# A four-layer attention network on one Trainium2 core: in layer 0 the product with v and the output projection take turns by steps, and the product for the sums moves one step behind GpSimd's addition

## The chip, the cores and the metric

The kernel runs on one core of a Trainium2 chip. The core has five engines that work side by side: TensorE (PE in the profile, its weight loads PEld), VectorE (DVE), ScalarE (ACT), GpSimd (POOL) and SyncE (SP, which here only issues transfers). Each runs its own instructions in the order of the program and waits where it needs the result of another. The metric is the device time in microseconds of one execution. The kernel before has a median of 2780.14 us in three runs.

## What is computed

A batch of four images with 512 channels and 32 x 32 pixels (1024 tokens) passes through four residual layers. Layers 0 and 2 are attention, layer 1 a gate per channel, layer 3 a lookup of the eight nearest rows of a table. The change is in layer 0, for each image:

```python
q, k, v = w_q @ gn(x), w_k @ gn(x), w_v @ gn(x)          # 8 heads of 64 channels
attn = einsum('bhdq,bhdT->bhqT', q, k) * scale           # scores per head
attn = einsum('gh,bhqT->bgqT', w_head, attn)             # mix the heads
attn = softmax(attn, axis=-1)
attn = (attn - mean) / sqrt(var + EPS) * gamma + beta    # norm of each head's whole map
out = einsum('bhqT,bhdT->bhqd', attn, v)
out = out.reshape(b, t, c) @ w_proj.T + b_proj
x = x + out
```

All data are 32-bit floats.

## The kernel before

**Steps.** Layer 0 walks over the images b = 0 to 3, and each image over steps s (the function `step`). An image has STEPS = 32 blocks of 32 queries. Step s does four things on four different blocks: it multiplies q and k for block s (`scores`, L425, in two halves), mixes the heads of block s - 2 (`mix`, L445), takes the exponent and turns it (`exps` L452, `turn_keys` L458), and multiplies with v a group of four blocks that lies LAG = 6 steps back (`apply`, L485). An image runs 38 steps: 32, and six in which only the later stages go on while the next image's q is projected. With `j, part = divmod(s - 6, 4)` a group j of four blocks (128 queries) is multiplied with v in the four steps part = 0 to 3: a quarter of the keys in each, all into the PSUM bank `pv`. After part 3 `take_out` (L548, ACT) copies the bank out.

**The relay.** Between scores and mix the rows must change partitions. After the second half of the scores ACT has copied them to `ss` (L431), and eight transfers, four issued by SP and four by GpSimd (L438), carry them to `s2`, which the mix two steps later reads. The page calls this transfer s<-ss.

**The sums.** The softmax denominators come from statistics that DVE takes of every exponent tile (`reduce`, bn_stats at L474). For a group j the generator `sums` does, in this order, one stretch per call of `next`: GpSimd adds up the statistics (L506); TensorE multiplies by the constant matrix `same`, which sums over partitions (L509), and DVE takes the reciprocal `ri` (L512); GpSimd stores `ri` to DRAM (L517) and checks its range; GpSimd loads it back spread over the partitions as `rb` (L525) and squares the statistics; GpSimd finishes the sum of squares `ssq`. The generator is held in `I["tail"]`. Before, the calls fall in part 0 at the head of the step, part 0 after the scores, and the ends of parts 0, 1 and 2. At the end of part 3 the generator `scale` starts: GpSimd multiplies the copied bank by `rb` (L561, half at the end of part 3, half at the end of the next part 0), and SP stores the result at the end of the next part 1.

**The projection of the image before.** While image b > 0 is in steps OUT = 12 to 27, `piece` projects the output of image b - 1: `put_quarter` makes in each step 256 columns of one of four row blocks (four matmuls at L658), DVE adds bias and residual (`add_to`, L624), and every second quarter closes a piece of 512 columns (`piece_done`, L640). 16 quarters make an image. The image's rows come by `image_piece` in odd steps and leave by `piece_out` in even steps.

**One shared bank.** `small_ps` always returns the same PSUM bank, pt. The projection of v (`take_v`, steps 0 to 6), the row sum of v (`sum_v`, L395 in step 7 and L405 in step 8), the product for the sums, the output projection, the statistics of the next image (`prepare` through `group_coeffs_parts`, L140 and L150) and the gate of layer 1 (`gating`, L815 and others, from step 28) all use it in turn; each waits until the one before has been read out.

**Order.** Nearly every instruction goes through `pin`, which keeps the order of the program on its engine. So the order of TensorE in a step is the order of the calls in `step`: scores, mix, scores, then (part 0) the product for the sums, `mid` (which calls sum_v, prepare or gating), `apply`, `piece`.

Of the kernel before, what the change touches and what calls it, by code (L numbers as in the profile page):

```python
# [16 lines left out]
P = 128  # L17
# [5 lines left out]
NB = 512  # L23
# [18 lines left out]
def fast_net(ctx: ExitStack, tc: tile.TileContext, a: dict, out: bass.AP, flag: bass.AP):  # L42
# [13 lines left out]
    def pin(ins):  # L56

        return tc.keep_in_program_order(ins)

    def small_ps(name):  # L60
        return pt_bank
# [154 lines left out]
    LAG = 6  # L216
# [151 lines left out]
    def take_k(b, m, at):  # L368
        I = img[b]
        if m == 0:  # L370
            I["k"] = big("k", f"k0_{b}")
        project(I["w_k"], tokens(I["xn"]), m, at,
                lambda ps: pin(nc.vector.tensor_copy(
                    I["k"][:, m, :].rearrange("p (t b j) -> p t j b", t=4, j=NS),
                    ps.rearrange("p (t j b) -> p t j b", t=4, j=NS))))

    def take_v(b, t):

        I = img[b]
        if t == 0:  # L380
            I["v"] = big("v", f"v0_{b}").rearrange("p k (i c) -> p (k i) c", c=C)
        ps = small_ps(f"v_{b}_{t}")
        for k in range(KC):
            pin(nc.tensor.matmul(  # L384
                ps, I["xn"][:, k, t::TC], I["w_v"][:, k, :],
                start=(k == 0), stop=(k == KC - 1),
            ))
        pin(nc.scalar.copy(I["v"][:, t, :], ps))
# [25 lines left out]
    def scores(b, s, n):  # L414


        I = img[b]
        q, k_ = I["q"], I["k"]
        if n == 0:
            I["ss", s] = eight_k([P, 2, T], f"ss_{b}_{s}", s % 2)  # L420
        ss = I["ss", s]
        sc = pairs["sc"]
        for m in range(KC):
            for r in range(2):
                pin(nc.tensor.matmul(  # L425
                    sc[m * NS:(m + 1) * NS, r, :],
                    q[r * HD:(r + 1) * HD, m, s * NS:(s + 1) * NS],
                    k_[r * HD:(r + 1) * HD, m, n * NB:(n + 1) * NB],
                    start=True, stop=True,
                ))  # L430
        pin(nc.scalar.copy(ss[:, :, n * NB:(n + 1) * NB], sc))  # L431
        if n == 0:
            return
        s2 = I["s2", s] = apool.tile([P, 2, T], F32, tag="s2", bufs=2, name=f"s2_{b}_{s}")
        del I["ss", s]
        for m in range(KC):
            for r in range(2):
                pin(relays[r].dma_start(  # L438
                    out=s2[r * KC + m::NH], in_=ss[m * NS:(m + 1) * NS, r, :]))

    def mix(b, s):
        s2 = img[b].pop(("s2", s))
        for t in range(4):
            for r in range(4):
                pin(nc.tensor.matmul(  # L445
                    pairs[f"mx{r // 2}"][t * NS:(t + 1) * NS, r % 2, :].rearrange("p (qq k) -> p qq k", qq=2),
                    wmix[r * NS:(r + 1) * NS], s2[r * NS:(r + 1) * NS, :, t * NK:(t + 1) * NK],
                    start=True, stop=True,
                ))

    def exps(s, half):
        pin(nc.scalar.activation(  # L452
            e[:, half].rearrange("p r qq k -> p (r qq k)"), flat2(pairs[f"mx{half}"]), AF.Exp))

    def turn_keys(s, half):

        j, i = divmod(s, 4)
        pin(nc.vector.transpose(  # L458
            eT[:, j % 2].rearrange("p b (qq i r) x -> p i r qq b x", qq=2, i=4)[
                :, i, 2 * half:2 * half + 2],  # L460
            e[:, half].rearrange("p r qq (b x) -> p r qq b x", x=NS),
        ))
# [10 lines left out]
                for qq in range(2):  # L473
                    pin(nc.vector.bn_stats(st[:, i, 2 * half + r, qq, :], e[:, half, r, qq, :]))  # L474

    def apply(b, s):

        I = img[b]
        j, part = divmod(s, 4)
        pv = pv_bank.rearrange("p (gp q) -> p gp q", q=P)  # L480
        for t in (2 * part, 2 * part + 1):
            for gp in range(KC):
                for r in range(2):
                    g = 2 * gp + r
                    pin(nc.tensor.matmul(  # L485
                        pv[r * HD:(r + 1) * HD, gp, :],
                        I["v"][:, t, g * HD:(g + 1) * HD],
                        eT[:, j % 2, t, :, 4 * g:4 * g + 4],
                        start=(t == 0 and gp == 0), stop=(t == TC - 1),
                        skip_group_check=True,  # L490
                    ))
# [54 lines left out]
    def take_out(b, j):  # L546
        pv = img[b]["pv"] = apool.tile([P, KC, P], F32, tag="o1", name=f"pv_{b}_{j}")
        pin(nc.scalar.copy(pv.rearrange("p gp q -> p (gp q)"), pv_bank))  # L548
# [66 lines left out]
    def out_view(b):  # L615
        return img[b]["of"].rearrange("p (j k g x) -> p k g j x", j=TC, g=NH, x=NS // 2)
# [6 lines left out]
    def add_to(b, m, xr, ps):  # L623
        pin(nc.vector.scalar_tensor_tensor(  # L624
            xr, ps, bproj[:, m:m + 1], xr, ALU.add, ALU.add))
# [5 lines left out]
    def piece_done(b, m, n):  # L631

        I = img[b]
        xr = I["xr", m, n]
        if n == 0:
            I["stb"] = small.tile([P, 2, 6], F32, tag="bnst", name=f"st_b{b}_{m}")
        if n == 0 and m == 0:
            I["mv"] = small.tile([P, KC, 2], F32, tag="mv", name=f"mv_b{b}")
        st, mv = I["stb"], I["mv"]
        pin(nc.vector.bn_stats(st[:, n, :], xr))  # L640
        if n == 0:
            return
        pin(nc.vector.bn_aggr(mv[:, m, :], st.rearrange("p i s -> p (i s)")))
        if m == KC - 1:
            mv1 = I["mv1"] = const.tile([P, 2, KC], F32, tag=f"mv1_{b}", name=f"mv1_{b}")
            pin(nc.vector.tensor_copy(mv1[:, 0, :], mv[:, :, 0]))
            pin(nc.vector.tensor_copy(mv1[:, 1, :], mv[:, :, 1]))

    def put_quarter(b, i):


        I = img[b]
        m, n4 = divmod(i, 4)
        Q = NB // 2
        ps = small_ps(f"p_{b}_{i}")[:, 0:Q]
        o = out_view(b)
        for k in range(KC):
            pin(nc.tensor.matmul(  # L658
                ps, I["w_p"][:, k, m * P:(m + 1) * P], o[:, k, 2 * n4:2 * n4 + 2],
                start=(k == 0), stop=(k == KC - 1),  # L660
            ))
        add_to(b, m, I["xr", m, n4 // 2][:, n4 % 2 * Q:(n4 % 2 + 1) * Q], ps)
        if n4 % 2:
            piece_done(b, m, n4 // 2)

    def put_out(b, m, at):

# [454 lines left out]
    for m, at in enumerate(("mx1", "sc", "mx0", "mx1")):  # L1122
        take_k(0, m, at)

    def step(b, s, mid, piece):


        I = img[b]
        old = s - 2
        j, part = divmod(s - LAG, 4)  # L1130
        tiled = 0 <= j < TC
        if tiled and part == 0:
            I["tail"] = sums(b, j)
            next(I["tail"])
        if s == 0:
            take_v(b, 0)
        if s < STEPS:
            scores(b, s, 0)
            early(b, s)
        if 0 <= old < STEPS:  # L1140
            mix(b, old)
            exps(old, 0)
            turn_keys(old, 0)
        elif s < STEPS:
            piece(b, s)
        if s < STEPS:
            scores(b, s, 1)
        if 0 <= old < STEPS:
            exps(old, 1)
        if tiled and part == 0:  # L1150
            next(I["tail"])
        mid(b, s)
        if tiled:
            apply(b, s - LAG)
            if part == 3:
                take_out(b, j)
        if 0 <= old < STEPS:
            turn_keys(old, 1)
            reduce(b, old)
        if old >= 0:  # L1160
            piece(b, s)
        if tiled and part < 3:
            next(I["tail"], None)
        if tiled and part < 2 and j > 0:
            next(I["scale"])
        if tiled and part == 3:
            I["scale"] = scale(b, j)
            next(I["scale"])

    OUT, NEXT = 12, 28
    state = {"behind": iter(()), "load": iter(())}

    def early(b, s):

        if b > 0 and s == TC - 1:
            state["load"] = collect(b - 1, False)
        if s == NEXT:
            state["load"] = (  # L1180
                next_image(0, "Wq", x1[0]) if b + 1 == B else next_image(b + 1, "w_q", x_v[b + 1]))
        next(state["load"], None)
# [22 lines left out]
    def piece(b, s):  # L1205
        if s < TC - 1:
            take_v(b, s + 1)
        elif b > 0 and OUT <= s < OUT + 16:
            put_quarter(b - 1, s - OUT)
        if TC < s < NEXT - 3 and not state["held"]:  # L1210
            state["held"] = next(state["ahead"]) is True

    for b in range(B):
# [4 lines left out]
        for s in range(STEPS):  # L1218
            step(b, s, mid, piece)
# [85 lines left out]
    for s in range(len(tiles) + 3):  # L1305
        if s < len(tiles):
            b, tt = tiles[s]
# [735 lines left out]
```

## Time and profile before

| what | value |
|---|---|
| median of three runs | 2780.14 us (2775.45 to 2785.22) |
| span of the profiled execution | 2784.4 us |
| TensorE busy over the span | 2614.6 us, 94% |
| stretch 465 to 580 us (image 1, steps with the projection): PE, DVE, ACT, POOL busy of 115 us | 111.68, 96.73, 66.80, 67.07 |
| the same stretch: share of the DMA engines, rate | 0.81, 211 GB/s |
| stretch 130 to 330 us (image 0, steps 6 and on, no projection): PE, DVE, ACT, POOL busy of 200 us | 178.19, 149.16, 115.81, 122.87 |
| the same stretch: share of the DMA engines, rate | 0.73, 190 GB/s |

The page's shares over the whole span mix four layers. For a change in layer 0 one reads the stretches of layer 0 (roughly 76 to 1310 us) and asks in each what the next matmul waited for. An fp32 matmul shows as two records, so "x8" in a line of L658 is four matmuls. A transfer's row shows its issue; when it landed is seen only in the chain of waits, from the instruction that it released.

### The profile page before, as it was taken

The numbers are of one execution on the slowest core, as the hardware profiler recorded it, in microseconds if no ns is written. First come the engines' busy times: TensorE is split into PE (matmuls) and PEld (weight loads), VectorE is DVE, ScalarE is ACT, GpSimd is POOL, SyncE is SP. The second block draws the span as 40 slices with busy tenths as digits, with TensorE's granted clock in tenths as the row PEclk, the third lists the DMA queues.
The fourth block names the chain that finished last, engine by engine and source line by source line (L and its number), as shares of the span: only waits on it lengthen the run. The fifth ranks groups of instructions, "written<-read, shape, count | busy, mean of one in ns | idle before, by whom it ended". The sixth has DMA issues, their size and how long they took to land.

```text
span 2784.4 us, 46982 instructions
## 1 busy us (share of the span) xinstructions
PE 2614.6 (94%) x18286; PEld 1170.4 (42%) x18286; DVE 1530.0 (55%) x2407; ACT 1003.6 (36%) x1128; POOL 1253.2 (45%) x1947
## 2 busy tenths in 40 slices
PE   7998998989989898989999999999999999999995
PEld 3443444545445443545433433343343334444442
DVE  4488347871578426872245234514623446888876
ACT  0465336551565325551154024214502532121210
POOL 2266415552456415562066026305601635666664
PEclk9999999999999999999999999999999999999997
DMA  2477438880687537784300030021002006766665
GB/s 77 107 205 205 140 90 213 218 214 27 161 222 209 151 82 196 194 216 173 127 18 1 31 121 1 16 76 60 1 30 91 1 28 192 217 185 213 186 185 149
DMA packets 159321, 349.82 MB, mean 126 GB/s; under 512 B 32361, under 2 KB 65129, under 8 KB 155378
## 3 DMA queue, kind: packets, MB, share of 16 engines
q1 hardware_dynamic: 86304, 167.04, 20.8%
q0 software_dynamic: 51200, 142.93, 19.0%
q10 hardware_dynamic: 21586, 36.76, 4.6%
q8 instruction: 147, 2.41, 0.4%
q14 instruction: 84, 0.69, 0.1%
HBM read 178.57 MB, written 33.69 MB: 76 GB/s over the span
## 4 chain that ended last, share of the span: by engine, by line
PE 74%; DMA 9%; ACT 6%; DVE 4%; POOL 4%; issue 3%; SPq 1%; ACTq 0%; POOLq 0%; DVEq 0%
PE at L1057 16%; PE mx L183 7%; PE sc L425 7%; PE pv_c L971 6%; PE pv L485 6%; PE sc_c L939 5%; DMA s<-ss 5%; PE pt L384 4%; PE sc L183 4%; ACT ss L431 3%; PE k L183 3%; PE v L195 3%; PE q L183 3%; PE p L183 3%; PE pt L658 3%
## 5 line engine op out<-in xcount | busy, mean ns | idle before, releaser
L458 DVE STREAM_TRANSPOSE eT<-e 128x1024 f32<-128x1024 f32 x256 | 317.4, 1242 | 278.5 <-ACT e L452 276.6
L438 POOL DMA_DIRECT2D s<-ss x512 | 260.4, 516 | 391.0 <-ACT ss L431 316.0
L947 ACT ACTIVATE eT<-sc_c 128x1024 f32<-128x1024 f32 x256 | 248.1, 1021 | 359.2 <-PE sc_c L939 357.2
L1074 POOL DMA_INDIRECT got<-in_mem,ix x256 | 278.9, 1089 | 209.9 <-issue 113.0
L431 ACT COPY ss<-sc 128x1024 f32<-128x1024 f32 x256 | 258.9, 1011 | 262.0 <-PE sc L425 203.0
L474 DVE BATCH_NORM_STATS2 st<-e 128x6 f32<-128x256 f32 x1024 | 341.6, 406 | 0.0
L425 PE MATMUL sc<-k,q 64*32 64x512 f32 x4096 | 286.3, 614 | 21.5 <-ACT ss L431 16.3
L955 POOL TENSOR_TENSOR e<-eT 128x1024 f32<-128x1024 f32 x96 | 232.4, 2423 | 149.3 <-ACT eT L947 139.0
L452 ACT ACTIVATE e<-mx 128x1024 f32<-128x1024 f32 x256 | 262.5, 1028 | 69.6 <-PE mx L445 35.8
L956 DVE TENSOR_TENSOR eT<-eT,e 128x1024 f32<-128x1024 f32 x96 | 143.5, 1494 | 236.3 <-POOL e L955 236.1
L485 PE MATMUL pv<-eT,v 128*64 128x128 f32 x4096 | 258.9, 281 | 0.0
L939 PE MATMUL sc_c<-q,k 64*128 64x512 f32 x1024 | 254.4, 615 | 3.7 <-DVE xr L624 2.3
L485 PEld LDWEIGHTS pv<-eT,v 128*64 128x64 f32 x4096 | 228.5, 140 | 62.1 <-issue 60.5
L971 PE MATMUL pv_c<-eT,v 128*64 128x512 f32 x1024 | 248.1, 605 | 2.8 <-ACT eT L947 2.8
L445 PE MATMUL mx<-s,wmix 32*32 32x512 f32 x4096 | 160.5, 630 | 51.1 <-DMA s<-ss 50.0
L1098 DVE SCALAR_TENSOR_TENSOR acc<-got,et,acc 128x512 f32<-128x512 f32 x224 | 168.5, 752 | 8.0
L996 DVE RECIPROCAL ri_c<-ri_c 128x512 f32<-128x512 f32 x32 | 107.2, 3351 | 112.5 <-ACT ri_c L995 112.5
L939 PEld LDWEIGHTS sc_c<-q,k 64*128 64x128 f32 x1024 | 88.3, 186 | 152.4 <-issue 127.6
L952 POOL TENSOR_TENSOR eT<-eT 128x1024 f32<-128x1024 f32 x32 | 78.9, 2466 | 146.2 <-ACT eT L947 146.2
L1000 POOL DMA_DIRECT2D fcw<-ri_c x64 | 33.3, 522 | 247.3 <-DVE ri_c L996 243.0
L561 POOL TENSOR_TENSOR o<-pv,rb 64x256 f32<-64x256 f32 x128 | 111.4, 870 | 73.3 <-ACT pv L548 66.4
L1062 ACT COPY att<-at 128x1024 f32<-128x1024 f32 x64 | 64.8, 1012 | 217.7 <-PE at L1057 194.4
(314 smaller groups left out, 3336.2 us busy)
## 6 DMA issues: line engine op xcount, KB each, us to landing
s<-ss SPq DMA_DIRECT2D x512, 128.0 KB
s<-ss POOLq DMA_DIRECT2D x512, 128.0 KB
rb<-r POOLq DMA_DIRECT2D x64, 128.0 KB
o<-o SPq DMA_DIRECT2D x32, 256.0 KB
xr<-in_x ACTq DMA_DIRECT2D x32, 256.0 KB
x<-xr SPq DMA_DIRECT2D x32, 256.0 KB
xr_c<-x SPq DMA_DIRECT2D x32, 256.0 KB
x<-xr_c SPq DMA_DIRECT2D x32, 256.0 KB
```

The costliest lines, as they stand in the source:

```text
L183: pin(nc.tensor.matmul(ps[:, n, :], w[:, k, m * P:(m + 1) * P], rhs(k, n), start=(k == 0), stop=(k == KC - 1),))
L425: pin(nc.tensor.matmul(sc[m * NS:(m + 1) * NS, r, :], q[r * HD:(r + 1) * HD, m, s * NS:(s + 1) * NS], k_[r * HD:(r + 1) * HD, m, n * NB:(n ...
L431: pin(nc.scalar.copy(ss[:, :, n * NB:(n + 1) * NB], sc))
L438: pin(relays[r].dma_start(out=s2[r * KC + m::NH], in_=ss[m * NS:(m + 1) * NS, r, :]))
L452: pin(nc.scalar.activation(e[:, half].rearrange("p r qq k -> p (r qq k)"), flat2(pairs[f"mx{half}"]), AF.Exp))
L458: pin(nc.vector.transpose(eT[:, j % 2].rearrange("p b (qq i r) x -> p i r qq b x", qq=2, i=4)[:, i, 2 * half:2 * half + 2], e[:, half].rea ...
L474: pin(nc.vector.bn_stats(st[:, i, 2 * half + r, qq, :], e[:, half, r, qq, :]))
L485: pin(nc.tensor.matmul(pv[r * HD:(r + 1) * HD, gp, :], I["v"][:, t, g * HD:(g + 1) * HD], eT[:, j % 2, t, :, 4 * g:4 * g + 4], start=(t == ...
L939: pin(nc.tensor.matmul(sc[:, r, :], I["k"][r * HD:(r + 1) * HD, m, t * P:(t + 1) * P], I["q"][r * HD:(r + 1) * HD, m, n * NB:(n + 1) * NB] ...
L971: pin(nc.tensor.matmul(pv[r * HD:(r + 1) * HD, :], I["v"][:, t, h * HD:(h + 1) * HD], e[:, r, :], start=(t == 0), stop=(t == TC - 1),))
L1057: pin(nc.tensor.matmul(sc[:, n * NB:(n + 1) * NB], xn3[b][:, k, tt * P:(tt + 1) * P], memT[k][:, i0:i0 + NB], start=(k == 0), stop=(k == K ...
L1074: pin(nc.gpsimd.indirect_dma_start(out=got[:, i, :], out_offset=None, in_=a["mem"], in_offset=bass.IndirectOffsetOnAxis(ap=ix[:, i:i + 1], ...
```

## The change

Two edits, both in the order of work and in the size of one product.

In steps 12 to 27 of images 1 to 3 the product with v and the projection no longer share each step. The projection is done in even steps with a whole piece of 512 columns (`put_half`, eight per image), and the product with v in odd steps, two quarters of the keys at once. The aim is fewer and larger matmuls for the same projection with no step longer than the others.

In all images the product for the sums moves from part 0 to part 1, a step behind GpSimd's addition, so that TensorE need not wait for it. The calls after it move by one step too: the store of `ri` and the check to the end of part 1, the load of `rb` to the end of part 2, the last of the squares to the end of part 3. `scale` stays where it was.

```diff
-    def apply(b, s):
+    def apply(b, j, parts):
         I = img[b]
-        j, part = divmod(s, 4)
         pv = pv_bank.rearrange("p (gp q) -> p gp q", q=P)
-        for t in (2 * part, 2 * part + 1):
+        for t in range(2 * parts.start, 2 * parts.stop):
...
-    def put_quarter(b, i):
+    def put_half(b, i):
         I = img[b]
-        m, n4 = divmod(i, 4)
-        Q = NB // 2
-        ps = small_ps(f"p_{b}_{i}")[:, 0:Q]
+        m, n = divmod(i, 2)
+        ps = small_ps(f"p_{b}_{i}")
         o = out_view(b)
         for k in range(KC):
             pin(nc.tensor.matmul(
-                ps, I["w_p"][:, k, m * P:(m + 1) * P], o[:, k, 2 * n4:2 * n4 + 2],
+                ps, I["w_p"][:, k, m * P:(m + 1) * P], o[:, k, 4 * n:4 * n + 4],
                 start=(k == 0), stop=(k == KC - 1),
             ))
-        add_to(b, m, I["xr", m, n4 // 2][:, n4 % 2 * Q:(n4 % 2 + 1) * Q], ps)
-        if n4 % 2:
-            piece_done(b, m, n4 // 2)
+        add_to(b, m, I["xr", m, n], ps)
+        piece_done(b, m, n)
...
-        if tiled and part == 0:
+        if tiled and part == 1:
             next(I["tail"])
         mid(b, s)
         if tiled:
-            apply(b, s - LAG)
+            if not (b > 0 and OUT <= s < OUT + 16):
+                apply(b, j, range(part, part + 1))
+            elif part % 2:
+                apply(b, j, range(part - 1, part + 1))
             if part == 3:
                 take_out(b, j)
...
-        if tiled and part < 3:
+        if tiled and part > 0:
             next(I["tail"], None)
...
-        elif b > 0 and OUT <= s < OUT + 16:
-            put_quarter(b - 1, s - OUT)
+        elif b > 0 and OUT <= s < OUT + 16 and s % 2 == 0:
+            put_half(b - 1, (s - OUT) // 2)
```

More of the change, by code (lines that the diff above doesn't have):

```diff
@@ L1123, in fast_net @@
         take_k(0, m, at)
+    OUT, NEXT = 12, 28
     def step(b, s, mid, piece):
@@ L1168, in step @@
             next(I["scale"])
-    OUT, NEXT = 12, 28
     state = {"behind": iter(()), "load": iter(())}
```

## The prediction

> **What bounds the kernel now.** First the page's busy shares and its chain, then the table of what TensorE waited for, then single steps of layer 0.
>
> ```profile
> PE 2614.6 (94%) x18286; PEld 1170.4 (42%) x18286; DVE 1530.0 (55%) x2407; ACT 1003.6 (36%) x1128; POOL 1253.2 (45%) x1947
> PE 74%; DMA 9%; ACT 6%; DVE 4%; POOL 4%; issue 3%; SPq 1%; ACTq 0%; POOLq 0%; DVEq 0%
> ```
>
> TensorE is the bound nearly everywhere, so a change is worth the TensorE work it removes plus the TensorE waits it removes, less the waits it makes. The waits of TensorE over the whole run (sum in us, times, longest):
>
> ```profile
> PE mx L445 <- DMA s<-ss: 50.0, 17, 6.6
> PE pt L509 <- POOL sums L506: 11.5, 11, 2.2
> PE pt L815 <- DVE ri L512: 2.4, 3, 1.5
> PE pt L150 <- DVE ri L512: 1.4, 3, 0.5
> ```
>
> The second line is the aim of the second edit: 11.5 us. The last two come from the same product: it holds bank pt, and the gate's matmul behind it must wait for the reciprocal.
>
> The chain in image 1, one step with a projection (start, us, work):
>
> ```profile
> 492.23 1.10 PE sc L425 x16
> 493.35 1.02 ACT ss L431
> 494.37 0.04 issue
> 494.42 1.09 PE sc L425 x16
> 495.51 1.90 PE pv L485 x32
> 497.41 1.92 PE pt L658 x8
> 499.33 1.10 PE sc L425 x16
> ```
>
> The step lasts 499.33 - 492.23 = 7.10 us and has no gap: the copy of the scores lies under the mix. The stretch 465 to 580 is 97% TensorE (111.68 of 115). Here removed TensorE work counts in full.
>
> The chain in image 0, where there is no projection:
>
> ```profile
> 157.60 2.60 DVE st L474 x8
> 160.37 0.27 POOL sums L506
> 160.68 0.41 PE pt L509 x2
> ...
> 169.75 6.02 DMA s<-ss
> 175.77 0.14 issue
> 175.91 1.26 PE mx L445 x30
> ```
>
> In part 0 the product waits for the addition, and that for DVE's statistics of the step before: the step from 156.11 to 162.91 lasts 6.8 us where its neighbour (150.93 to 156.11) lasts 5.2. But three steps on the mix waits too, for the relay of part 1. These two waits alternate in every group of image 0 (products at 160.68, 184.49, 208.06, mixes at 175.91, 199.48, 223.64). So removing the first may lengthen the second.
>
> [...]
>
> **The change, part by part.**
>
> A. Projection, three images. Removed: 48 quarters at 1.92 us (four matmuls of 256 columns). Added: 24 halves. The same strided operand with 512 columns is in the last image's projection:
>
> ```profile
> 1360.33 6.87 PE mx L183 x16
> 1367.20 6.87 PE sc L183 x16
> ```
>
> 6.87 us for two halves, 3.44 each. A pair of steps goes from 3.84 to 3.44, and 24 x 0.40 = **-9.7 us**. The products with v only move: 1.90 twice in the odd step. New steps: even 3.26 (scores, mix, scores) + 3.44 = 6.70, odd 3.26 + 3.80 = 7.06, so they stay level, and the next scores still have over 3 us for their copy. DVE: 24 additions at 0.75 (the L624 rows with 128x512) for 48 at 0.467: 18.0 for 22.4 us. ACT copies `pv` 1.9 us later within the step; the bank is next written more than a step later. Nothing for either.
>
> B. The wait for the addition. It gets a whole step, 5 to 7 us, against a longest wait of 2.2, and falls to about 0. By the timeline 7.3 of the 11.5 us are in image 0, 4.2 in the others. What comes back is bounded by 0 and all of it. In image 0 the relay of part 1 decides: it is slow (6.0 us against 3.2 to 4.4 in image 1) because two 128 KB loads of `rb` and the store of o go out behind it (169.73 and 170.92). The edit moves `rb` to part 2, so that relay should speed up. I take two thirds, **-5**; for the others **-2.5**.
>
> C. The 3.8 us of the gate. Its matmuls at L150 and L815 fall in part 0 steps (30 and 34); the product now falls in 31 and 35, where the gate uses GpSimd. **-2.5**, between 0 and -3.8.
>
> D. New conflicts in pt, where `mid` of a part 1 step uses the bank right behind the product, with no product with v between to hide the reciprocal. Step 7: `sum_v`. In image 0 now:
>
> ```profile
> 139.30 3.59 PE L395 MATMUL pt<-w_v,ybar 128*1 128x512 f32 x8
> 139.43 1.25 DVE L458 STREAM_TRANSPOSE eT<-e 128x1024 f32<-128x1024 f32 x1 [3.42 <-ACT e L452]
> ```
>
> The product would take 139.29 to 139.63, but the reciprocal stands behind the transpose on DVE (to 140.68) and takes 0.32 (L512): sum_v starts near 141.0, 1.4 us late. Behind it queue the product with v and the next scores, hence the relay. Four images, 5.6 us; since in images 1 to 3 the copy of the scores then waits for transfers anyway (1.75 us at 447.51), **+4.5**. Step 27: the second matmul of `prepare` (L150), again 1.4 to 2 us in four images, 0 to +7. In image 0 the mix at 277.66 waits 3.63 us for the relay issued just ahead of this stall, which hides it: **+1.5**.
>
> E. `rb` a step later. Issued at the end of part 2 (8.1 us into the step, as at 169.73 + 1.28 for the step of 162.91), needed by GpSimd's multiplication about 13 us into it (157.76 for the step of 144.72): 4.9 us. Landing: [...]at most some 6.3 like the slowest relay of those groups (6.34 at 217.06 in the chain). So GpSimd stalls 0 to 1.4 us per group; behind it stand the addition and four relay issues. They have 1.3 us of room (multiplications to 159.6, addition 0.3, relay at 161.22). **+0.5**.
>
> F. The product for the sums now follows a half's addition by one step. DVE does it after the statistics, 9.2 us into the even step, to 9.95; the product is due at 6.70 + 3.29 = 9.99. Twelve products with 0.1 us or less each: **+1**, up to +4 if DVE lags, as its even step grows: two transposes 2.5, statistics 2.67, addition 0.75, statistics of the piece and of the next image 0.69 each, about 7.4 us; the odd one has 5.5. Together 12.9 in 13.8, so it catches up.
>
> Sum: -9.7 - 5 - 2.5 - 2.5 + 4.5 + 1.5 + 0.5 + 1 = -12.2, so **2768 us**.
>
> **The rivals.**
> 1. Image 0 is held by the relay and all stalls count: A -9.7, B 0 and -1, C -1.5, D +5.6 and +5, E +1, F +2 = +1.4, **2782**. For it: the alternating waits. Against: the relay has a cause that moves.
> 2. All waits go and the stalls hide: -9.7 - 11.5 - 3.8 + 3 = -22, **2758**. Against: D at step 7 has nothing to hide it in image 0.
> 3. Slower: DVE's even steps or a late `rb` hold up relays and exponents. With half a us in each of the 32 groups, less the gains of A and C: +16 + 5.6 - 9.7 - 2.5 = +9.4, **2790**. For it: DMA at 0.81 of its time at 211 GB/s, DVE at 84%. Against: no relay wait of TensorE in the full steps of image 1.
>
> **How the numbers follow.** My sum 0.50, rival 1 0.24, rival 2 0.13, rival 3 0.13. Predicted is the first. The range 2757 to 2783 holds the first three but for their tails. The bound of 0.3% is 8.3 us, 2771.8 below and 2788.5 above. Faster: three quarters of the first case, rival 2 and a few of rival 1, 0.55. Slower: two thirds of rival 3 and a few of rival 1, 0.13. Same: 0.32.
>
> **What would show it.** A: L656 with 192 records, 3.4 us per half, pairs of steps at 13.8 where they were 14.2. B: the line of the wait for POOL sums gone, step of part 0 in image 0 at 5.2; if right, the wait of the mix for the relay in image 0 grows by less than 3 us. C and D: waits behind the reciprocal gone at L812, new at L395 (four of 1.4) and at L150 in step 27. E: no stall of L561 on a transfer. F: no wait of the product for the half's addition. Wrong if the pairs stay at 14.2, if the relay wait grows by what B frees, or if step 7 costs more than 2 us.

## The result, and the profile after

The change makes the kernel slower. Times are medians in us, each beside runs of the kernel before on the same chip; the ratio is after over before, with its 95% interval.

| series | after | before | ratio |
|---|---|---|---|
| first | 2804.07 (6 runs) | 2778.48 (6 runs) | 1.0080 [1.0056, 1.0104] |
| repeated later, code unaltered | 2798.83 (8 runs) | 2782.27 (53 runs) | 1.0054 [1.0036, 1.0073] |

The forecast was 2768 us in a range of 2757 to 2783. All six times lie above the range. Single runs of one kernel scatter by 4 to 6 us (standard deviation) and go with the mean clock granted to TensorE (some 2 us for each 0.001 in the kernel before, whose runs have 0.976 to 0.986), so below a stage is compared over two profiles of each kernel where two exist.

The two figures that head the page, busy time of each engine and the shares of the chain that ended last:

```profile
PE 2621.7 (94%) x18094; PEld 1145.2 (41%) x18094; DVE 1523.5 (54%) x2383; ACT 1003.0 (36%) x1128; POOL 1250.4 (45%) x1947
PE 76%; DMA 9%; DVE 4%; ACT 4%; POOL 3%; issue 3%; SPq 1%; ACTq 0%; DVEq 0%; POOLq 0%
```

TensorE has 192 records fewer (the halves) and yet 7 us more busy time: 2621.7 for 2614.6. Work was removed, so some of what stayed must have run slower. The engine's waits (sum, times, longest) tell a second thing:

```profile
PE mx L445 <- DMA s<-ss: 53.6, 23, 5.1
PE pt L150 <- DVE ri L511: 7.8, 4, 2.0
PE pt L395 <- DVE ri L511: 7.4, 4, 2.6
PE pt L140 <- DVE mv_a L341: 3.1, 3, 1.3
```

Lines up to L474 keep their numbers; later ones have moved up by one to three (L484, L508, L511, L656 and L812 were L485, L509, L512, L658 and L815). The wait for GpSimd's sums (11.5 us) and the gate's behind the reciprocal (2.4 us at L812) are gone. In their place stand 15.2 us behind the same reciprocal in just two steps: at sum_v (L395, step 7) and at the second matmul of prepare (L150, step 27).

Where the time went, by steps, from the starts of TensorE's first scores in each (us, sum over the four images, mean of two profiles of each kernel, spans 2784.4 and 2780.3 before, 2803.4 and 2793.8 after):

| part of the run | before | after | difference |
|---|---|---|---|
| ahead of step 0 of image 0 | 84.4 | 83.2 | -1.2 |
| steps 0 to 6 | 210.9 | 209.5 | -1.3 |
| step 7 | 34.8 | 48.6 | +13.8 |
| steps 8 to 11 | 112.2 | 113.9 | +1.7 |
| steps 12 to 26 | 426.2 | 412.0 | -14.2 |
| step 27 | 28.7 | 40.3 | +11.6 |
| step 28 to the next image's step 0 (images 0 to 2) | 323.1 | 329.0 | +5.9 |
| from step 28 of image 3 to the end | 1562.1 | 1561.9 | -0.1 |

The gain that the change was made for is there, 14.2 us in steps 12 to 26 (two profiles of one kernel differ by 3 us there). Eight steps out of 128 cost 25.4.

The full steps first. The timeline of TensorE in image 1 of the kernel after (start, us, work):

```profile
490.34 3.70 PE L656 MATMUL pt<-of,w_p 128*128 128x512 f32 x8
493.97 1.09 PE L425 MATMUL sc<-k,q 64*32 64x512 f32 x16
...
497.25 0.41 PE L508 MATMUL pt<-sums,same 128*128 128x32 f32 x2
497.59 3.71 PE L484 MATMUL pv<-eT,v 128*64 128x128 f32 x64
501.23 1.09 PE L425 MATMUL sc<-k,q 64*32 64x512 f32 x16
```

The half stands from 490.34 to 493.97, 3.63 us; the next step has both quarters of v, 3.64, and in part 1 the product, 0.34. No record shows an idle time before it.

Step 7 of image 1, from the timeline of all engines, other instructions left out:

```profile
431.41 2.41 ACTq L248 DMA_DIRECT2D of<-o  x3
...
433.49 0.41 PE L508 MATMUL pt<-sums,same 128*128 128x32 f32 x2
433.94 1.02 ACT L452 ACTIVATE e<-mx 128x1024 f32<-128x1024 f32 x1 [1.53 <-PE pt L508]
435.00 1.25 DVE L458 STREAM_TRANSPOSE eT<-e 128x1024 f32<-128x1024 f32 x1 [4.46 <-ACT e L452]
...
436.17 0.32 DVE L511 RECIPROCAL ri<-pt 128x32 f32<-128x32 f32 x1
436.54 5.29 PE L395 MATMUL pt<-w_v_n,ybar 128*1 128x512 f32 x8 [2.64 <-DVE ri L511]
```

Read it from the end. sum_v waits 2.64 us for the reciprocal; the reciprocal stands on DVE behind the transpose of the exponent; the transpose waits for the exponent; and the exponent starts at 433.94, when ACT has issued the three loads of the image before (431.41 + 2.41 = 433.82; "ACTq" marks an issue). The bracket behind the exponent names the product, which ended at the same time; the experiment on the loads below decides between the two. Then sum_v takes 5.29 us, where before it took 3.59 for the same eight records.

Step 27 of image 1, TensorE alone:

```profile
583.76 0.41 PE L508 MATMUL pt<-sums,same 128*128 128x32 f32 x2
586.17 0.39 PE L150 MATMUL pt<-gsq_a,gavg 128*128 128x4 f32 x2 [2.00 <-DVE ri L511]
586.48 5.38 PE L484 MATMUL pv<-eT,v 128*64 128x128 f32 x64
```

The same picture: a wait of 2.00 us, then 5.38 us for what took 3.71 at 497.59. What slows the work behind a stop is in the table of windows (window, length, busy time of PE, PEld, DVE, ACT, POOL, then granted clock, DMA share, GB/s). Rows: step 7 of image 0, step 7 of image 1, step 27 of image 1:

```profile
136.25:146.64 10.39, 9.07 (x108) 3.27 (x107) 3.61 (x7) 4.56 (x5) 3.54 (x9) 1.00 0.51 131
430.21:443.66 13.45, 10.76 (x108) 3.44 (x107) 3.60 (x6) 4.45 (x5) 3.51 (x9) 0.87 0.63 167
580.48:591.79 11.31, 9.27 (x133) 6.38 (x132) 9.43 (x25) 3.97 (x4) 5.81 (x12) 0.85 0.79 207
```

In image 0 the clock is 1.00 through the step, and its length is the forecast's: 8.71 before, plus the product of 0.34, plus a wait of 1.27. In image 1 the mean clock falls to 0.87: TensorE is busy 1.7 us longer with the same 108 records. This is the busy time that the head of the page shows.

### The profile page after: what moved, and what is told of

Its sections match the earlier page's. It is cut to its first block, busy times and chain, and to the rows that moved or that the text cites. A ratio compares the mean times of both kernels' runs of the same rounds, so it can differ in the third digit from the quotient of the medians.

```text
span 2803.4 us, 46602 instructions
## 1 busy us (share of the span) xinstructions
PE 2621.7 (94%) x18094; PEld 1145.2 (41%) x18094; DVE 1523.5 (54%) x2383; ACT 1003.0 (36%) x1128; POOL 1250.4 (45%) x1947
## 4 chain that ended last, share of the span: by engine, by line
PE 76%; DMA 9%; DVE 4%; ACT 4%; POOL 3%; issue 3%; SPq 1%; ACTq 0%; DVEq 0%; POOLq 0%
PE at L1054 16%; PE mx L183 7%; PE sc L425 6%; PE pv_c L968 6%; PE sc_c L936 6%; PE pv L484 5%; DMA s<-ss 5%; PE pt L384 4%; PE sc L183 4%; PE p L183 3%; PE k L183 3%; PE v L195 3%; PE q L183 3%; PE pt L656 3%; PE mx L445 2%
## 5 line engine op out<-in xcount | busy, mean ns | idle before, releaser
L474 DVE BATCH_NORM_STATS2 st<-e 128x6 f32<-128x256 f32 x1024 | 341.6, 406 | 0.0
L452 ACT ACTIVATE e<-mx 128x1024 f32<-128x1024 f32 x256 | 262.4, 1028 | 82.6 <-PE mx L445 41.2
L484 PE MATMUL pv<-eT,v 128*64 128x128 f32 x4096 | 260.0, 285 | 0.0
L484 PEld LDWEIGHTS pv<-eT,v 128*64 128x64 f32 x4096 | 235.3, 143 | 46.7 <-issue 41.0
L445 PE MATMUL mx<-s,wmix 32*32 32x512 f32 x4096 | 160.4, 633 | 58.4 <-DMA s<-ss 53.6
L968 PEld LDWEIGHTS pv_c<-eT,v 128*64 128x64 f32 x1024 | 65.1, 137 | 170.9 <-issue 148.9
```

Source lines behind the costliest of these rows:

```text
L452: pin(nc.scalar.activation(e[:, half].rearrange("p r qq k -> p (r qq k)"), flat2(pairs[f"mx{half}"]), AF.Exp))
L484: pin(nc.tensor.matmul(pv[r * HD:(r + 1) * HD, gp, :], I["v"][:, t, g * HD:(g + 1) * HD], eT[:, j % 2, t, :, 4 * g:4 * g + 4], start=(t == ...
L968: pin(nc.tensor.matmul(pv[r * HD:(r + 1) * HD, :], I["v"][:, t, h * HD:(h + 1) * HD], e[:, r, :], start=(t == 0), stop=(t == TC - 1),))
```

## Experiments

The explanation under test is that the slowdown comes from two stops, product and next user of pt back to back in steps 7 and 27, with what a stop does to the clock. Its rivals: the halves themselves are slow (DVE's larger additions, late pieces), or rb a step later delays GpSimd's multiplication and with it the relays. Where nothing else is said, an edit is made to the kernel after. Each series shares its runs of the kernel before: 2780.48 for the first four, 2782.27 for the next four, 2782.22 for the last three.

**Halves alone.** The product and the calls after it go back to part 0:

```diff
-        if tiled and part == 1:
+        if tiled and part == 0:
...
-        if tiled and part > 0:
+        if tiled and part < 3:
```

> The projection in halves, taking turns with the product with v, but the sums as before (product in part 0, calls after it not shifted). Theory 1 (the loss of the changed kernel is TensorE standing still behind the product for the sums, in steps 7 and 27, and a lower TensorE clock after each such stop): steps 7 and 27 are as before, 8.7 us and 7.4 us in images 1 to 3; but in the 12 part 0 steps of the projection a half now stands right behind the product and waits about 1.3 us for the reciprocal, so -9 for the larger matmuls, +16 for these waits, in all 2780 to 2795. Theory 2 (the later load of rb holds up GpSimd and the relay): rb is as before, so 2765 to 2772. Theory 3 (the alternation loads VectorE's even steps and slows the steps of the projection): as slow as the changed kernel, 2795 to 2810, and pairs of steps longer than 14.2 us.

Measured: 2789.29, ratio 1.0027 [1.0015, 1.0040]. Step 7 is back at 34.8 and step 27 at 27.2, but steps 12 to 26 take 439.7, 13 more than before. Waits of TensorE:

```profile
PE pt L656 <- DVE ri L511: 12.2, 12, 1.3
PE pt L508 <- POOL sums L505: 11.9, 10, 2.4
```

Twelve times the half stands right behind the product in an even step of part 0, and waits about 1.0 us each, up to 1.3, for the reciprocal: that step lasts 8.59 us where the change with both edits has 6.92. In the kernel before, the quarter of v stood between the two. So the halves need the shift of the product, and a neighbour of the product without v between pays in any step, not only in steps 7 and 27.

**Shift alone.** The kernel before with quarters, and only this:

```diff
-        if tiled and part == 0:
+        if tiled and part == 1:
             next(I["tail"])
...
-        if tiled and part < 3:
+        if tiled and part > 0:
             next(I["tail"], None)
```

> The product for the sums one step later with all that follows it, the projection in quarters as before. Theory 1: the whole loss is here and the gain of the larger matmuls is missing: step 7 at 12 to 13 us in images 1 to 3 and step 27 at 9.5 to 11.5, 2800 to 2815, that is slower than the changed kernel by up to 9. Theory 2: also slow, 2800 to 2815, but with steps 7 and 27 near the old times and the loss spread over the groups. Theory 3: 2770 to 2782.

Measured: 2799.98, ratio 1.0052 [1.0026, 1.0077], the same slowdown as the whole change. Step 7 takes 46.5 and step 27 35.0; steps 12 to 26 take 418.2, 8 less than before. Its waits:

```profile
PE pt L395 <- DVE ri L512: 6.7, 4, 2.4
PE pt L150 <- DVE ri L512: 5.6, 4, 1.8
```

The wait for GpSimd's sums shrinks to 0.5 us, one time. Step 27 stays under the 9.5 to 11.5 us expected (9.10 in images 1 to 3): its stops there are 1.27 us, and v behind them takes 1.97, as it does without a stop. The slowdown belongs to the shift; the halves are not needed for it.

**v ahead of mid.** In part 1 the product with v goes between the product for the sums and `mid`. Halves, shift and late rb stay:

```diff
-        mid(b, s)
+        if not (tiled and part == 1):
+            mid(b, s)
         if tiled:
...
+            if part == 1:
+                mid(b, s)
             if part == 3:
```

> The changed kernel, but in part 1 steps the product with v goes ahead of mid, so that it stands between the product for the sums and sum_v (step 7) or the matmul of prepare (step 27), while VectorE takes the reciprocal. Nothing else is moved. Theory 1: the waits behind the reciprocal fall from 7.4 + 7.8 us to under 3, step 7 back to 9 us and step 27 to about 7.5, the clock stays up in both, 2762 to 2775, faster than the kernel before. Theories 2 and 3: no more than 5 us better than the changed kernel, 2790 to 2805.

Measured: 2778.36, ratio 0.9983 [0.9973, 0.9993]. The steps came as expected, 36.8 for step 7 and 28.6 for step 27; the whole did not quite reach the 2762 to 2775 expected. Step 7 of image 1 on TensorE:

```profile
421.73 0.41 PE L508 MATMUL pt<-sums,same 128*128 128x32 f32 x2
422.06 1.97 PE L484 MATMUL pv<-eT,v 128*64 128x128 f32 x32
424.60 3.59 PE L395 MATMUL pt<-w_v_n,ybar 128*1 128x512 f32 x8 [0.57 <-DVE ri L511]
```

The reciprocal is as late as before, but 1.90 us of v cover it all but 0.57, and sum_v is back at 3.59. The order of two calls in one part takes the whole slowdown away with the halves and the late rb still there. That rejects both rivals as causes of the slowdown.

**v ahead in step 7 only.** The same edit under `s == TC - 1`, so that step 27 keeps its stop.

> The same edit in step 7 alone: the wait in step 27 stays. Theory 1: about half of what the edit in all part 1 steps brings, 12 us of some 26 by the lengths of the steps, so 2780 to 2794; step 27 at 9.5 to 11.5 us as in the changed kernel. A rival within theory 1, that the clock matters and not the waits: no gain where a stop of under 1 us is left. Theories 2 and 3: as the changed kernel, 2795 to 2807.

Measured: 2786.36, ratio 1.0015 [1.0004, 1.0027]. Step 7 takes 37.1, step 27 42.0. Of the waits behind the reciprocal the table keeps almost only this one:

```profile
PE pt L150 <- DVE ri L511: 7.8, 4, 2.0
```

So the ratio goes from 1.0080 or 1.0054 to 1.0015 with step 7 mended, and to 0.9983 with step 27 mended too. Step 7 is worth 11 to 18 us, step 27 about 9.

**The three loads to SP.** The stops stay, but the three loads in step 7 are issued by SP instead of ACT:

```diff
-        yield from in_threes([(of[:, j], o_rows[b][:, j]) for j in range(6)])
+        for j in range(3):
+            pin(nc.sync.dma_start(out=of[:, j], in_=o_rows[b][:, j]))
+        yield
+        yield from in_threes([(of[:, j], o_rows[b][:, j]) for j in range(3, 6)])
```

> The changed kernel, but the first three loads of the image before (of<-o), which ACT issues in step 7 ahead of its copy of the scores, are issued by SP. Theory 1a (in images 1 to 3 the reciprocal of step 7 is late because ACT's issue of 2.4 us delays the exponent and so the transpose that stands ahead of it; the stop then lowers the clock): the wait of L395 falls from 1.5 to 2.6 us to about 1.3 as in image 0, where the row sum of v ran at full clock (3.6 us, not 5.3); if the clock holds at 1.3, step 7 is 10.4 us in all four images, 2 to 3 us less in each of three. If the clock falls at 1.3 us too, step 7 is near 12.1 us. Rival (the wait of step 7 has another cause, such as the relay): no change of the wait. Total 2790 to 2802.

Measured: 2789.91, ratio 1.0020 [1.0010, 1.0029], beside 1.0054 for the kernel after in the same series. Step 7 of image 1:

```profile
427.16 0.41 PE L508 MATMUL pt<-sums,same 128*128 128x32 f32 x2
428.84 3.59 PE L395 MATMUL pt<-w_v_n,ybar 128*1 128x512 f32 x8 [1.27 <-DVE ri L511]
```

All four images now have the step of image 0: 10.38 us, a wait of 1.27, sum_v at 3.59. The exponent starts 2.36 us into the step, where it started 3.73 us into it in the kernel after above. So these loads made the difference between image 0 and the others, in the wait and through it in sum_v, which takes 3.59 for up to 5.29: 48.3 us for step 7 became 41.5. (Step 27, without an edit, gave 42.8 for 39.4 in the kernel after of that series: behind its stop of 2.00 us in image 1 v took 6.59 for 3.71.)

**v ahead in every step**, and **both edits**. The first puts `apply` ahead of `mid` in all parts (the copy of the bank stays behind `mid`), the second adds the loads to SP.

```diff
-        mid(b, s)
         if tiled:
...
-            if part == 3:
-                take_out(b, j)
+        mid(b, s)
+        if tiled and part == 3:
+            take_out(b, j)
```

> The changed kernel with the product with v ahead of mid in every step, not in part 1 alone; only the bank's copy stays behind mid. Theory 1: as with the edit in part 1 steps (2778), and where the matmul of prepare in step 25 now waits 1.3 us for the next image's statistics (VectorE's even step has grown), the product with v fills that too: step 25 from 8.6 to about 7.3 us in images 1 and 2, 2774 to 2779. If step 25 was held by something else, no difference to 2778.

> Both edits: v ahead of mid in every step, and the first loads issued by SP. Theory 1: the rest of the wait in step 7 of images 1 to 3 (about 0.7 us in step 7 of image 1) goes too; 2772 to 2778, faster than the kernel before by 0.1 to 0.3%. If SP's issue delays its half of the relay instead, 2778 to 2784.

Measured: 2778.19, ratio 0.9988 [0.9974, 1.0003], and 2779.98, 0.9990 [0.9979, 1.0000]. Neither beats the narrower edit. Step 25 of images 1 and 2 does shorten as expected, from 8.58 to 7.24 us (7.58 before), and the wait of L140 for the statistics of the next image (mv_a) is gone. That gain is more than given back in step 31: there the product now waits 1.85 us for GpSimd's addition in each of the images 1 to 3, 5.6 us in all. With v in front, the time no longer shows who issues the loads; that SP's issue delays its half of the relay does not show either (steps 8 to 11 take 109.0 for 109.3).

**The product behind v, at the end of the step.** The other way to part the neighbours: `mid` stays ahead of v, and the product moves behind it.

```diff
-        if tiled and part == 1:
-            next(I["tail"])
         mid(b, s)
...
             reduce(b, old)
+        if tiled and part == 1:
+            next(I["tail"])
```

> Theory 1 by another way: the changed kernel, but the product for the sums itself goes to the end of the part 1 step, behind mid and the product with v, and its reciprocal behind VectorE's statistics. Nothing in the step uses the bank after it. Step 7 at 9 us, step 27 at 7.5, no wait for the reciprocal in either, 2772 to 2782. If what helped was not the missing wait but that v comes early, 2790 to 2805.

Measured: 2779.72, ratio 0.9988 [0.9975, 1.0001]. Step 7 takes 36.2 with no wait behind the reciprocal in any image, step 27 28.6. Two different orders without the neighbourhood give the same time.

**Repeats.** The kernel after, the kernel before and the kernel with v ahead of mid in part 1 ran again in later series.

> The changed kernel unaltered, beside the others on one chip, and for a second profile. All theories: 2790 to 2808. If the clock is part of the loss, its time goes with the mean clock of a run, about 2 us for each 0.001, and the row sums of v that run at half clock in this profile are those of steps after a stop, not the same ones in every run.

> The kernel before, unaltered, for a second profile: how far two profiles of one kernel differ stage by stage. If the steps 12 to 26 of images 1 to 3 are bound by TensorE, they agree within 3 us of 332; the steps near the loads of the next image (8 to 11 and 28 to 31) may differ by 5 us and more, since their waits are for transfers.

> The changed kernel with v ahead of mid in part 1 steps, once more, for a second profile and more runs. Theory 1: 2774 to 2781, 0.1 to 0.3% below the kernel before. Steps 12 to 26 of images 1 to 3 again 8 us or so below the kernel before; where the total is less than that below, the difference must stand in the steps bound by transfers, 8 to 11 and 28 to the next image, or in image 0.

Measured: 1.0054 [1.0036, 1.0073] for the kernel after, 0.9994 [0.9981, 1.0007] for the kernel before against itself, and 2776.15, 0.9987 [0.9976, 0.9998], for v ahead of mid. The last is faster than both kernels of this case, and than the kernel before by 2.1 and 6.1 us in its two series. Two profiles of the kernel before agree in steps 12 to 26 of images 1 to 3 as expected (332.1 and 331.5); v ahead of mid has 324.5 and 328.7 there, so the 8 us expected came once and 3 us the other time.

That is less than its steps promise. In the last series both profiled runs lie at the median of their kernel (2782.07 before, 2775.92 with v ahead): image 3's step 28 starts 10.3 us earlier (1210.0 for 1220.3), but the rest of the run, where nothing was edited, takes 1564.2 for 1560.1. The first profile of the kernel before has 1564.1 there, so this part moves by 4 us of itself. How much of the 10 us the later layers really give back stays open.

## Why the prediction was wrong

**A, the projection (forecast -9.7): right.** A pair of steps is 6.92 + 6.93 = 13.85 us, as forecast (13.8), for 14.22. That the sum fits is luck in part, for two terms were off and cancel: a half takes 3.63 instead of 3.44, two quarters of v in a row 3.64 instead of 3.80. In images 1 to 3 steps 12 to 26 went from 331.8 to 322.7 (means of two profiles), -9.1. This sum also holds B's share of these images and a cost that the forecast lacked: step 25 is longer by 1 us in two images, through DVE's later statistics.

**B, the wait for the addition (forecast -5 and -2.5): right.** It is gone but for one wait of 1.3 us in the second profile. The relay did not take it all back: image 0's steps 8 to 26 went from 117.8 to 112.4, -5.4 (two profiles of the kernel before differ by 3.5 there), and the shift alone shortened steps 12 to 26 of images 1 to 3 by 2.7. The mix waits 2 to 4 us longer in the whole run (53.6 and 52.4 for 50.0 and 50.2).

**C, the gate (forecast -2.5): wrong.** The waits behind the reciprocal at L812 are gone, but from step 28 to the next image the kernel after takes 329.0 for 323.1. The shift alone takes 323.9 there, the halves alone 328.5, v ahead of mid 324.5 and 325.7. In no version do they take less than the 322.0 of the second profile of the kernel before (324.1 in the first), so no gain of C shows; why they lengthen in some was not settled.

**D, the product next to mid (forecast +4.5 and +1.5): this is the step that failed.** It named the two right places and the right mechanism, and sized them at 6 us. Beyond the moved product, both steps together cost about 24 (48.6 + 40.3 for 36.2 + 28.6 in the version with the product behind v). Three terms were mis-sized or missing.

1. "sum_v starts near 141.0, 1.4 us late", times four. Image 0 gave 1.27. That image is the only one with no loads on ACT in step 7; the other three waited 2.64, 1.94 and 1.53. One image was costed and multiplied by four; what else is queued on the engines ahead of the reciprocal was left out.
2. What follows a stop was costed at its usual duration. In images 1 to 3 sum_v took 5.29 for 3.59, three times 1.7, at a mean granted clock of 0.68 in each; in step 27 v took 5.38 and 5.28 for 3.71, and 3.19 for 1.97 in image 0. Step 7 comes to 7.4 of waits and 5.1 of clock, step 27 to 7.8 and 4.5. Versions without the stops have 36.2 and 28.6, so 36.2 + 12.5 = 48.7 and 28.6 + 12.3 = 40.9 against 48.9 and 41.2 in the first profile. Over all runs of the later series the mean clock is 0.978 in the kernel after and 0.981 in the kernel before.
3. "In image 0 the mix at 277.66 waits 3.63 us for the relay, which hides it." The stop was 1.83 to 2.00 us in all four images, the most that was forecast, but it was not hidden: image 0's steps 27 to 30 take 32.4 and 32.6 us for 29.4 and 29.6 before, and 30.6 and 30.8 with v ahead of mid.

The first of the three could be read from the kernel before, in step 7 of image 1:

```profile
426.80 2.15 ACTq L248 DMA_DIRECT2D of<-o  x3
428.88 3.59 PE L395 MATMUL pt<-w_v_n,ybar 128*1 128x512 f32 x8
430.13 1.25 DVE L458 STREAM_TRANSPOSE eT<-e 128x1024 f32<-128x1024 f32 x1 [4.55 <-ACT e L452]
```

The sum that was made for image 0 gives 430.13 + 1.25 + 0.32 = 431.70 here for the end of the reciprocal and 428.88 + 0.34 = 429.22 for that of the product: a wait of 2.5 us, where 2.64 was measured. The discount for the wait at 447.51 rests on the same oversight: that copy of the scores stands behind an exponent that follows ACT's issue of one load (w_p, 443.20 to 445.41).

**E and F (+0.5, +1): right.** GpSimd waited for rb once per profile, 0.5 and 1.1 us. Landings of rb took 2.9 to 8.5 us, median 5.0, more than the 6.3 at most of the forecast, with room enough. No wait of the product for a half's addition shows; what DVE's fuller even step did cost is step 25, above.

Put together, A and B gave what they should, the steps of C ended some 8 us off and D some 19 us, and these two alone turn the -12 into the +16 of the profiles. **Rival 3** ended on the right side for another reason: DVE's even steps and late rb were present in the version with v ahead of mid, which is not slower. **Rival 1** took the stalls of step 7 and 27 at their full length, 10.6 us, and still had no term for the clock or for the loads.

Behind stops of one length the second term came or did not. Step 27 of the kernel after stops for 2.00 us in image 1 and in image 3; the product with v that follows (window, length, busy time of PE, then granted clock, DMA share, GB/s):

```profile
586.48:591.86 5.38, 5.38 (x73) 0.68 0.89 224
1237.65:1241.36 3.71, 3.71 (x73) 1.00 0.93 228
```

The same 73 records take 5.38 us at a mean clock of 0.68 in image 1 and 3.71 at 1.00 in image 3. In the second profile, behind stops of 1.99 and 2.00 us, they take 3.71 in images 1 and 2 and 5.12 in image 3. What decides between the two was not shown. In steps 7 and 27 of the profiles of this case there are ten stops of 1.27 us, and none was followed by longer work (sum_v at 3.59 or 3.60, v at 1.97). Of the five stops of 1.53 us in step 7, four were (sum_v at 5.29) and one, in the shift alone, was not (3.59).

## What to carry to other kernels

When a product and the next user of its bank come to stand side by side, the reading engine's whole queue lies between them: go through every instruction ahead of the read on that engine and on the one that feeds it, DMA issues included (here 2.41 us of them on ACT, and a wait of 2.64 us for 1.27), in each image and not in one. Keep an independent matmul between the two, here 1.9 us of v; that one order was worth 20 us or so, more than the gain that the change was made for. A stop of TensorE near 2 us may be charged twice, once as a wait and once as slower work behind it, and the busy time of the page shows the second. It need not be: of the stops near 2.00 us in step 27 of images 1 to 3, two were in one profile of the kernel after (v at 5.38 and 5.28 for 3.71) and one in the other (5.12), so two runs of one kernel need not pay for the same stops.

## What the runs showed of the hardware

- Behind a stop of 1.53 us in step 7 of image 3 of the kernel after, sum_v ran at a mean granted clock of 0.68 (0.50 at the lowest) and took 5.29 us. Behind one of 1.27 us in image 0 the clock was 1.00 and sum_v took 3.60.
- Three DMA issues on ACT, 2.41 us in all, let its exponent start 3.73 us into step 7 of image 1 instead of 2.36, and with it held DVE and TensorE two engines further on: the wait of sum_v was 2.64 us and the step 13.45, against 1.27 and 10.38 with the issues on SP.
- Executions of the kernel before on one chip differ by up to 26 us in 2780; its time falls by about 2 us for each 0.001 of mean clock (1.7 to 2.4 in fits to four sets of 18 to 62 runs). With 22 runs of a version and 50 to 60 of the kernel before, the 95% interval of their ratio is still 0.2% wide, some 5 us.
